# A four-layer image network on one core: layer 1 in pieces of 32 rows instead of 16, layer 0 in row pairs

## The chip, the cores and the metric

The kernel runs on one core of a Trainium2 chip. TensorE is PE here, VectorE is DVE, ScalarE is ACT, GpSimd is POOL; SyncE (SP) issues every transfer. PEld is PE's loading of weights. The metric is the device time of one execution in microseconds (us).

## The reference, cut to what matters

The input `x` has 8 images of 32 channels and 256 x 256 pixels, fp32. Four layers follow each other, and each has the form "x + layer(normalised x)", with a mean and a variance that the kernel gathers per channel or channel group over a whole image. So a layer of an image can't begin before the layer ahead of it has finished that image.

- Layer 0: a 1 x 1 convolution to `feat`, an average of `feat` over 5 x 5 regions, and a depthwise 5 x 5 convolution of `feat` with that average as its filter, zeros beyond the border. The kernel folds both convolutions into one 5 x 5 convolution of 32 x 32 channels, whose 25 taps differ by image.
- Layer 1, by far the largest: the input is normalised and rounded to whole numbers from -127 to 127 (`q`), and the output is a sum of absolute differences:

```
out[n, f, i, j] = -sum over c, kh, kw of | patch[n, c, i + kh, j + kw] - w[f, c, kh, kw] |     (3 x 3, 32 -> 32)
```

- Layer 2: a 3 x 3 convolution, 32 to 32 channels, with bias.
- Layer 3: four blocks of "FastKAN" (layernorm, 8 Gaussian bases per value, a matrix, plus SiLU times a matrix) on windows and on grids of pixels.

## The kernel before

**Layout.** An image's 256 rows are cut into 4 bands (`q` as an index, `NQ`) of 64 rows; a tile has 128 partitions, 32 channels of each band. A chunk `k` is 8 rows of each band; 8 chunks make an image.

**A planner writes the order.** The code does not issue instructions as it goes. Each step is a task with an engine, an estimated duration, the buffers that it reads and writes, and a rank; `Plan.run` plays all tasks and fixes the order on PE, DVE, ACT and SP before anything is issued. Each engine then works through its own list in that order. Layers of neighbouring images overlap: while layer 1 works on image b, layer 0 of image b + 1 and layers 2 and 3 of image b - 1 run beside it. `TURN`, `L0A`, `L0B`, `L3A`, `L3B` are the ranks, as fractions of an image.

**Layer 1** (`stage1`, `Pass`, `Parts`). Because |a - w| = 2 max(a - w, 0) - a + w, the sum splits into three. The large part is max(q - w, 0), one instruction per output channel and tap over all input channels: `Parts.distance`, on DVE at line 1133 (subtract, max) or, as a filler in ACT's gaps, at line 1135, where one ACT instruction makes half the rows. It writes a bf16 tile of kind `dv`, of which there are `NDV` = 3. PE then sums over the channels with a 128 x 32 selection matrix (`gather`, line 1155): eight matmuls of 512 columns, four side by side in the array. The second part is the box sum of q itself, the same for all outputs (also line 1155, source `qh`), nine gathers. The third is a constant, `wsum`.

A pass is one quarter of the rows of each band (`h`, `NH` = 4, `RH` = 16 rows) and one quarter of the outputs (`g`, `NG` = 4, `OG` = 8 outputs): 72 distances and 9 box-sum gathers into the accumulator `psA` (2 banks), to which PE adds the layer's own input with two fp32 identity matmuls (`residual`, line 1144). ACT evicts `psA` to `xr` (line 1202) and sums it; a second ACT instruction squares it (line 673) after a one-column shift on DVE (line 666). There is one `psA`, so the next pass's first gather waits for that eviction. There are 16 passes an image. `qh`, the rows of q with one more on each side, has two buffers of 18 rows, used in turn and loaded by SP (line 1174). `xr` is loaded (line 1193) and stored (line 1215) in four transfers of 128 KB.

**Layer 0** (`stage0`). For the first image alone a chunk is convolved with 32 x 32 tiles. For the others `one_block` loads one band's chunk four times (line 954), shifted by a row, a column and both, so that K = 128 holds 2 x 2 taps: nine taps (line 967) of four 128 x 32 fp32 matmuls into `psC`, one bank. DVE first clears the margins of the tile (lines 941 and 942). ACT evicts (line 989). There are 32 blocks an image, tiles of kind `x0`, 3 slots; if these are taken and enough of the shared `arena` is free, a block takes its tile there.

**Layers 2 and 3** use `psB` (4 banks) and groups of 16 matmuls of 32 x 32 tiles (`mm16`, line 631; layer 2 at line 1287; the scales of layer 3 at line 1426; variances at line 1394 with 128 x 32). Bases are made by ACT at lines 1530 and 1545 or by DVE at line 1535; they lie in `bas`, `arena` or, once layer 1 is over, `dv`. Where it serves, DVE does an eviction at line 1382.

Of the kernel before, what the change touches and what calls it, by code (L numbers as in the profile page):

```python
# [24 lines left out]
R = 8  # L25
# [23 lines left out]
KCOL = 7  # L49


C32, MG, MS, IDENT, MV, W0, CQ, RL, ONES, PAT = range(10)
NMAT = 10


EYE, CEN32, CEN16 = range(3)
VAR = 3
# [6 lines left out]
NSEL = 9 + W0T  # L64


BASE = 16 * (W + 2) // 2
XP = W + 4
XW = 12 * XP
NX = 3  # L70
NBAS, NSI = 2, 3
TURN = (0.05, 0, 0.12, 0.2, 0.071, 0.232, 0.274, 0.235, 0.5, 0.311, 0.737, 0.685, 0.891, 0.2)


def room():
    n = 13 * F + 3 * BASE - NBAS * BASE - NSI * F - NX * XW
    fixed = [("bas", NBAS * BASE, BASE), ("si", NSI * F, F), ("rs", F // 2, F // 4), ("xr", 3 * F // 4, 3 * F // 4)]
    return fixed + [("x0", NX * XW, XW), ("sb", n, 0)]

URGENT = 2  # L80
IDLE = 8.0
NDV = 3
SPARE = 512
WIDE_SPARE = 9216
BASE_SPARE = 0
HOLD = 1
L0A, L0B = -0.0321, 0.4065
L3A, L3B = 0.0072, 0.7303
# [6 lines left out]
NH = 4  # L95
RH = HB // NH
NG = 4
OG = C // NG
NJ = 4
NI = 2  # L100
# [19 lines left out]
class Plan:  # L120
# [57 lines left out]
    def fits(self, need, spare):  # L178
# [3 lines left out]
        for b in need:  # L182
            if b.kind in ("dv", "bas") and b.spill:
                b.kind = "dv" if self.places["dv"] else "bas"
# [208 lines left out]
class Pass:  # L393


    def __init__(self, plan, b, h, g, opened, parts):
        self.b, self.h, self.g, self.opened, self.parts = b, h, g, opened, parts
        self.terms = [(o, t) for t in range(9) for o in range(OG)]
        self.queue, self.rest = [], None
        self.sums = list(range(9))  # L400
        self.left = 9 + OG * 9
        self.ps = Buf("psA")
        self.ps.first, self.ps.left = self, 1
        self.added = self.done = False
        plan.passes.append(self)

    def piece(self, plan, e):

        if self.rest is None:
            d = Buf("dv")  # L410
            d.spill = self.b == 0
            if not plan.fits([d], 0):
                return None
            (o, t), lo = self.terms.pop(0), 0
            d.left = 3
        else:
            (o, t, d, lo), self.rest = self.rest, None
        hi = RH if e == "DVE" or lo else RH // 2
        if hi < RH:
            self.rest = o, t, d, hi  # L420
        elif not lo:
            d.left = 2

        def ended(_):
            d.made = getattr(d, "made", 0) + hi - lo
            if d.made == RH:
                self.queue.append((o, t, d))

        us = (0.13 + 1.075 * (hi - lo) / RH) if e == "DVE" else 0.12 + 3.575 * (hi - lo) / RH
        return plan.filler(e, us, lambda: self.parts.distance(self, e, d, o, t, lo, hi), [d], [d], ended)  # L430

    def on_pe(self, plan, urgent):
# [4 lines left out]
        late = (9 - len(self.sums)) * 9 < 9 * 9 - self.left or not (self.terms or self.rest or self.queue)  # L437
        if self.sums and len(self.queue) < URGENT and (late or not (urgent or self.queue)):
            t, us, bufs, n = self.sums.pop(0), 0.46, [], 1
            fn = lambda: self.parts.gather(self, None, None, t)  # L440
        elif self.queue and (len(self.queue) >= URGENT or not urgent):
            o, t, d = self.queue.pop(0)
            us, bufs, n = 0.46, [d], 1
            fn = lambda: self.parts.gather(self, d, o, t)
        elif not self.added and self.residual.over and (self.left < 20 or not urgent):
            us, bufs, n = 1.75, [], 0
# [18 lines left out]
def kernel(  # L465
# [26 lines left out]
    nc.sync.dma_start(tl[:, :W0T], sel[:, OG + 1 :])  # L492
# [31 lines left out]
    sel_b = const.tile([P, OG + 1, C], BF16, name="sel_b")  # L524
# [4 lines left out]
    with tc.tile_pool(name="prepp", bufs=2, space=PSUM) as ps:  # L529
# [7 lines left out]
        sel_f = prep((OG + 1) * C).rearrange("p (o c) -> p o c", c=C)  # L537
        nc.sync.dma_start(sel_f, sel[:, : OG + 1])
        nc.vector.tensor_copy(sel_b, sel_f)
        wi = prep(C * 9)  # L540
# [28 lines left out]
        nc.vector.memset(one_k, QSCALE)  # L569
        for g in range(NG):  # L570
            spread = prep(P)
            by_place = spread.rearrange("p (j o q) -> p o j q", j=NJ, o=OG)
            for i in range(NJ * NQ):
                nc.vector.tensor_copy(by_place[:, :, i // NQ, i % NQ], wo[:, g * OG : (g + 1) * OG])
# [7 lines left out]
    qh = [const.tile([P, RH + 2, W + 2], BF16, name=f"qh{i}") for i in range(2)]  # L582
    for i in range(2):
        nc.gpsimd.memset(qh[i][:, :, 0:1], 0.0)
        nc.gpsimd.memset(qh[i][:, :, W + 1 : W + 2], 0.0)
# [4 lines left out]
    tiny = const.tile([P, 350], F32, name="tiny")  # L590
    img = [
        {
            "x1": scratch.tile([NH, NJ, C, NQ, NI, 512], F32, name=f"x1_{b}"),
            "x2": scratch.tile([NH, NJ, C, NQ, NI, 512], F32, name=f"x2_{b}"),
# [42 lines left out]
    class Norm:  # L637


        def __init__(self, b, which, n, rank, last=None):  # L640
            at = 0 if which < 2 else 1 + b % 2
            t = tiny[:, at * 110 : at * 110 + 110]
            self.n, self.rank, self.last = n, rank, last
            self.mv = t[:, 68 : 68 + 2 * n].rearrange("p (n s) -> p n s", s=2)
            self.g = t[:, 76 : 76 + 2 * n].rearrange("p (n s) -> p n s", s=2)
            self.d = t[:, 84 : 84 + 2 * n].rearrange("p (n s) -> p n s", s=2)
            self.v = t[:, 92 : 92 + n]
            self.t = t[:, 96 : 96 + n]
            at = 330 + 2 * (5 * (b % 2) + which)
            self.m = tiny[:, at : at + 2]  # L650
            self.y = t[:, 104 : 104 + n]
# [4 lines left out]
            self.nsums = 2 * NH * n if n == 1 else NH * n  # L656
# [23 lines left out]
        def finish(self):  # L680
            n, average, last = self.n, MV if self.n > 1 else MG, self.last
# [3 lines left out]
            def first():  # L685
                mean, d, q = self.mv[:, :, 0], self.v, self.t
                for of, a, k in ((d, self.sums, self.nsums), (q, self.squares, 2 * NH * n if n == 1 else NH * n)):
# [8 lines left out]
            pv = lambda: psC[:, 0 : 2 * n].rearrange("p (n s) -> p n s", s=2)  # L696
# [17 lines left out]
            def third():  # L714
# [11 lines left out]
                if last is None:  # L726
                    nc.vector.tensor_copy(self.m, self.g[:, 0, :])

            plan.add("DVE", 2.8, third, r=[p], w=[small] + ([self.done] if last is None else []), rank=self.rank)
            if last is not None:  # L730

                p = Buf("psC")

                plan.add(
                    "PE", 0.6, lambda: nc.tensor.matmul(pv(), mat(last), self.g, start=True, stop=True),
                    r=[small], w=[p], rank=self.rank,
                )

                def fifth():
                    if n == 1:  # L740
                        nc.vector.tensor_copy(self.m, pv()[:, 0, :])
                        return
                    nc.vector.tensor_scalar(self.m, pv()[:, 0, :], col(GSEL), None, ALU.mult)
                    for i in range(1, n):
                        nc.vector.scalar_tensor_tensor(
# [1098 lines left out]
```

## Time and profile before

| | us |
|---|---|
| three runs, lowest, median, highest | 15038.8, 15039.77, 15045.56 |
| the profiled execution | 15035.73 |
| its span, first to last instruction | 15034.0 |
| DVE busy | 13135.5 |
| PE busy | 12664.4 |
| ACT busy | 11831.0 |
| HBM read and written, in MB | 1424.32 and 771.75 |

The page gives busy times of each engine over the span and the costliest groups of instructions: line, engine, operation, output and inputs, partitions x elements, count, then busy time in us and the mean of one in ns, then the engine's idle time ahead of them and what ended it. A view of waits lists who waited for whom, with total, number and longest. The windows view lists the stretch, its length, and busy time (and instructions) of PE, PEld, DVE, ACT and POOL, then the granted TensorE clock, the DMA share and GB/s. The timeline merges neighbouring instructions of a kind: start, duration, what, count, and in brackets the idle time before. A duration includes an end in which the next instruction may already have started, so a pace is read from start to start.

### The profile page before, as it was taken

The numbers are of one execution on the slowest core, as the hardware profiler recorded it, in microseconds if no ns is written. First come the engines' busy times: TensorE is split into PE (matmuls) and PEld (weight loads), VectorE is DVE, ScalarE is ACT, GpSimd is POOL, SyncE is SP. The second block draws the span as 40 slices with busy tenths as digits, with TensorE's granted clock in tenths as the row PEclk, the third lists the DMA queues.
The fourth block names the chain that finished last, engine by engine and source line by source line (L and its number), as shares of the span: only waits on it lengthen the run. The fifth ranks groups of instructions, "written<-read, shape, count | busy, mean of one in ns | idle before, by whom it ended". The sixth has DMA issues, their size and how long they took to land. (4 is left out here: it accounts for less than half of the span.)

```text
span 15034.0 us, 506670 instructions
## 1 busy us (share of the span) xinstructions
PE 12664.4 (84%) x231764; PEld 4345.4 (29%) x231764; DVE 13135.5 (87%) x12530; ACT 11831.0 (79%) x7586; POOL 32.3 (0%) x25
## 2 busy tenths in 40 slices
PE   6898978889878899889998899978998887866566
PEld 4333322223222232222332223322232222222122
DVE  1899899998999999999899998899989999975676
ACT  1899678896788868888688877888778888876567
POOL 0000000000000000000000000000000000000000
PEclk8999989999999999999999999989999999987677
DMA  4655566665766566765767658775677655455565
GB/s 120 120 131 119 132 158 152 144 147 136 175 157 148 139 144 156 175 157 142 172 161 181 158 123 182 178 172 132 149 170 181 145 127 122 125 143 132 144 149 134
DMA packets 2583263, 2229.00 MB, mean 148 GB/s; under 512 B 1436416, under 2 KB 2292992, under 8 KB 2506368
## 3 DMA queue, kind: packets, MB, share of 16 engines
q1 hardware_dynamic: 2581120, 2196.57, 61.8%
q8 instruction: 1815, 29.74, 0.9%
q14 instruction: 328, 2.69, 0.1%
HBM read 1424.32 MB, written 771.75 MB: 146 GB/s over the span
## 5 line engine op out<-in xcount | busy, mean ns | idle before, releaser
L1133 DVE TENSOR_SCALAR dv<-qh,w1q 128x4128 bf16<-128x4128 bf16 (+1 forms) x8897 | 10649.3, 1262 | 718.5 <-PE psA L1155 697.1
L1155 PE MATMUL psA<-dv,sel_b 128*32 128x512 bf16 x71304 | 5339.1, 393 | 1090.3 <-DVE dv L1133 858.5
L1155 PEld LDWEIGHTS <-sel_b 128*32 128x32 bf16 x82944 | 2128.1, 96 | 6106.5 <-issue 5138.8
L1530 ACT ACTIVATE bas<-arena,kb 128x2048 f32<-128x2048 f32 x1016 | 2009.2, 1996 | 449.9 <-PE psB L631 242.3
L967 PE MATMUL psC<-x,w 128*32 128x512 f32 x15768 | 1985.1, 596 | 21.1 <-ACT x L989 8.6
L1545 ACT ACTIVATE bas<-bas 128x2048 f32<-128x2048 f32 x1016 | 1926.9, 1899 | 0.4
L631 PE MATMUL psB<-bas,tl 32*32 32x512 f32 x35584 | 1424.9, 646 | 290.0 <-ACT bas L1545 99.5
L1135 ACT ACTIVATE dv<-qh,w1n 128x2064 bf16<-128x2064 bf16 x481 | 947.6, 2007 | 570.0 <-PE psA L1155 541.6
L1530 ACT ACTIVATE arena<-arena,kb 128x2048 f32<-128x2048 f32 x697 | 1388.5, 1993 | 4.9 <-DVE arena L1434 2.4
L1545 ACT ACTIVATE arena<-arena 128x2048 f32<-128x2048 f32 x697 | 1317.1, 1900 | 0.0
L631 PE MATMUL psB<-arena,tl 32*32 32x512 f32 x30240 | 1160.3, 609 | 104.3 <-ACT si L1618 49.5
L1434 DVE TENSOR_TENSOR arena<-psB,arena 128x2048 f32<-128x2048 f32 x280 | 639.7, 2284 | 149.9 <-PE psB L1426 147.6
L1618 ACT ACTIVATE si<-psB,cols_sb 128x2048 f32<-128x2048 f32 x189 | 371.4, 1965 | 501.3 <-PE psB L631 447.2
L1155 PE MATMUL psA<-qh,sel_b 128*32 128x512 bf16 x9216 | 677.7, 386 | 100.6 <-DMA qh<-q 84.4
L967 PEld LDWEIGHTS psC<-x,w 128*32 128x32 f32 x15768 | 501.6, 110 | 700.5 <-issue 401.7
L631 PEld LDWEIGHTS psB<-bas,tl 32*32 32x32 f32 x35584 | 360.9, 107 | 960.3 <-issue 425.1
L1377 ACT ACTIVATE arena<-psB 128x2048 f32<-128x2048 f32 x216 | 405.0, 1875 | 293.1 <-PE psB L631 292.9
L631 PE MATMUL psB<-si,tl 32*32 32x512 f32 x13984 | 608.7, 629 | 26.9 <-issue 7.0
L1287 PE MATMUL psB<-x,tl 32*32 32x510 f32 (+1 forms) x15360 | 584.9, 608 | 36.6 <-issue 36.5
L1385 ACT ACTIVATE arena<-arena 128x2048 f32<-128x2048 f32 x273 | 522.5, 1914 | 11.6 <-PE psV L1394 2.3
L1426 PE MATMUL psB<-rs,tl 32*32 32x512 f32 x8960 | 348.7, 641 | 145.2 <-DVE arena L1434 66.5
L631 PEld LDWEIGHTS psB<-arena,tl 32*32 32x32 f32 x30240 | 291.2, 103 | 549.5 <-issue 290.5
(211 smaller groups left out, 8697.1 us busy)
## 6 DMA issues: line engine op xcount, KB each, us to landing
x<-in_x_dram SPq DMA_DIRECT2D x850, 384.0 KB
arena<-y SPq DMA_DIRECT2D x128, 1024.0 KB
si<-sy SPq DMA_DIRECT2D x500, 256.0 KB
x<-x SPq DMA_DIRECT2D x492, 256.0 KB
x<-x SPq DMA_DIRECT2D x120, 1024.0 KB
arena<-x SPq DMA_DIRECT2D x68, 1024.0 KB
xr<-x SPq DMA_DIRECT2D x512, 128.0 KB
x<-xr SPq DMA_DIRECT2D x512, 128.0 KB
```

The lines of the kernel that those rows point to most:

```text
L631: nc.tensor.matmul(view(o[j * C : (j + 1) * C, i - first, :]), w_, src(rows, i, j), start=start, stop=stop)
L967: nc.tensor.matmul(psC[j * C : (j + 1) * C, :], w4[:, t, :], d[:, 2 * j + y : 2 * j + y + 2, z : z + W], start=t == 0, stop=False,)
L1133: nc.vector.tensor_scalar(dst, src, w1q[:, at : at + 1], 0.0, ALU.subtract, ALU.max)
L1135: nc.scalar.activation(dst, src, AF.Relu, bias=w1n[:, at : at + 1])
L1155: nc.tensor.matmul(psA[j * C : (j + 1) * C, i, :], sel_b[:, n, :], src[:, at : at + 2, t % 3 : t % 3 + W], **flags,)
L1287: nc.tensor.matmul(o[:, lo - 2 * j : hi - 2 * j, c0:c1], (wc if t == 4 else tl[:, W2T + t, :])[rows], d[rows, lo + dy + 1 : hi + dy + 1, c ...
L1377: lambda ps=ps, at=at: nc.scalar.activation(sb(c)[:, at], ps().rearrange("p s f -> p (s f)"), func, bias=shift),
L1385: square = plan.add("ACT", 1.82, lambda: nc.scalar.activation(sb(sq), sb(c), AF.Square), r=[c], w=[sq], rank=rk)
L1434: lambda ps=ps, at=at: nc.vector.tensor_tensor(sb(c)[:, at], ps().rearrange("p s f -> p (s f)"), sb(c)[:, at], ALU.mult),
L1530: lambda: nc.scalar.activation(sb(bas), sb(rb), AF.Square, bias=kb[:, n, k : k + 1]),
L1545: lambda: nc.scalar.activation(sb(bas), sb(bas), AF.Exp, scale=-1.0, bias=0.0 if sq.eng == "ACT" else kbsq[:, n, k : k + 1]),
L1618: nc.scalar.activation(sb(o), psB.rearrange("p s f -> p (s f)"), AF.Identity, bias=obias)
```

## The change

- Layer 1's piece is 32 rows (`NH` = 2, `RH` = 32) and two outputs (`NG` = 16, `OG` = 2): a distance is 8256 elements per partition, a gather 16 matmuls into one bank of `psA`, a pass 18 distances; there are 32 passes an image. `dv` has two tiles of 32 rows.
- q of a half image lies in one buffer of 34 rows, loaded in two parts. The last pass of a half image makes its distances rows 0 to 15 first, then 16 to 31; the first part of the load is released when the first are made, the second when all are. The first pass of the next half makes rows 0 to 13 first, then 14 to 31.
- The nine box sums are made once for each half image, into `psC`, and put away as two bf16 halves (`ss`, by ACT and by DVE). Each pass adds them with two bf16 identity matmuls beside the fp32 one for its input.
- Layer 0's block is one half of a chunk, two bands in two row groups of 64: each band's rows are loaded twice, shifted by one row, so K = 64 holds two rows of taps, and 15 taps of eight matmuls fill two banks of `psC`. The columns at the border are left out of the matmul instead of cleared in the tile; only blocks at the image's upper and lower border are still cleared.
- Outputs of layer 0 are kept in another channel order, so that a pass's two outputs lie where one transfer fetches or stores them; the sums of the norm are averaged and picked accordingly.
- `x0` has 2 slots, `bas` 1, `xr` 3 (of half the size); ranks and planner constants are set anew; ACT's piece as a filler stays 16 rows (`RA`), after `IDLE` = 16 us instead of 8.

```diff
-NX = 3
-NBAS, NSI = 2, 3
+NX = 2
+NBAS, NSI = 1, 3
-URGENT = 2
-IDLE = 8.0
-NDV = 3
+URGENT = 1
+IDLE = 16.0
+NDV = 2
+RA = 16
-NH = 4
+NH = 2
 RH = HB // NH
-NG = 4
+CUT = RH // 2
+NG = 16
 OG = C // NG
-NI = 2
+NI = 4
...
 def piece(self, plan, e):
-        hi = RH if e == "DVE" or lo else RH // 2
+        hi = z if e == "DVE" or lo > a else min(a + RA, z)
...
+            load = self.then[part]
+            if load is not None and not self.open[part]:
+                load.wait -= 1
...
 def one_block
-                for s in range(4):
-                    lo, hi = max(r0 - 2 + s // 2, 0), min(r0 + 10 + s // 2, H)
-                    nc.sync.dma_start(
-                        grid(slice(s * C, (s + 1) * C))[:, at : at + hi - lo, 2 - s % 2 : 2 - s % 2 + W], x[b, :, lo:hi, :]
-                    )
+                for n in range(4):
+                    i, s = divmod(n, 2)
+                    r0 = first(i) - 2 + s
+                    lo, hi = max(r0, 0), min(r0 + 12, H)
+                    rows = slice(n * C, (n + 1) * C)
+                    nc.sync.dma_start(
+                        sb(xt)[rows, (lo - r0) * W : (hi - r0) * W], x[b, :, lo:hi, :].rearrange("c r w -> c (r w)")
+                    )
...
+            if first(0) == 0 or first(1) + R == H:
+                plan.add("DVE", 0.6, clear, w=[xt], rank=rk - 0.03 * span, after=after)
...
                 for j in range(NJ):
-                    nc.tensor.matmul(
-                        psC[j * C : (j + 1) * C, :], w4[:, t, :], d[:, 2 * j + y : 2 * j + y + 2, z : z + W],
-                    )
+                    for i in range(2):
+                        rows = slice(i * 2 * C, (i + 1) * 2 * C)
+                        nc.tensor.matmul(
+                            o[:, :, c0:c1], w4[rows, t, :], grid(rows)[:, 2 * j + y : 2 * j + y + 2, c0 + dx : c1 + dx],
+                        )
...
 class Parts
-            src, dst = qh[ps.h % 2][:, t // 3 + lo : t // 3 + hi, :], place(d)[:, lo:hi, :]
+            src, dst = qh[:, t // 3 + lo : t // 3 + hi, :], place(d)[:, lo:hi, :]
...
         def residual(self, ps):
-            for i in range(NI):
-                nc.tensor.matmul(psA[:, i, :], mat(IDENT), sb(ps.xr)[:, i * 512 : (i + 1) * 512], **flags)
+            nc.tensor.matmul(psA, mat(IDENT), sb(ps.xr)[:, 0:FS], start=start, stop=False)
+            for i in range(2):
+                nc.tensor.matmul(psA, eye_b, halves(ps.ss, i), start=False, stop=stop and i == 1)
...
+        def total(self, h, t):
+            src = qh[:, t // 3 : t // 3 + RH, t % 3 : t % 3 + W]
+            for n, (j, w, v) in enumerate(by_unit(OG * NI, src)):
+                i = n // NJ
+                nc.tensor.matmul(psC[j * C : (j + 1) * C, 0], sel_b[:, w, :], v, ...)
...
 def stage1
+            for t in range(9):
+                plan.add("PE", 0.88, lambda h=h, t=t: Parts().total(h, t), r=qh_buf, w=[p], rank=b - SUMS)
+            plan.add("ACT", 0.57, lambda s=s: nc.scalar.activation(halves(s, 0), psC[:, 0], AF.Copy), r=[p], w=[s], ...)
+            low = plan.add("DVE", 0.7, lambda s=s: nc.vector.tensor_tensor(halves(s, 1), psC[:, 0], halves(s, 0), ALU.subtract), ...)
...
+                if g == 0 and (b or h):
+                    ps = Pass(plan, b, h, g, [loads[:1], loads[1:]], [0, CUT - 2, RH], Parts())
+                elif ends:
+                    ps = Pass(plan, b, h, g, [loads, loads], [0, CUT, RH], Parts())
+                else:
+                    ps = Pass(plan, b, h, g, [loads], [0, RH], Parts())
```

## The prediction

> **What bounds the kernel now.** I read the page first, then the busy time of each engine by stretches, the groups with shapes kept apart, the waits of DVE, and the timeline of a steady place.
>
> ```profile
> PE 12664.4 (84%) x231764; PEld 4345.4 (29%) x231764; DVE 13135.5 (87%) x12530; ACT 11831.0 (79%) x7586; POOL 32.3 (0%) x25
> ```
>
> No engine is full over the span, but the span has three parts: a start without layer 1 (0 to 425), eight images of layer 1 (425 to 13292), a tail with the last image's layers 2 and 3. In the middle:
>
> ```profile
> 2256.00:13160.00 10904.00, 9600.33 (x177656) 3119.22 (x177656) 10119.05 (x9356) 8937.41 (x5733) 24.71 (x13) 0.97 0.65 153
> 13292.00:15034.00 1742.00, 1084.76 (x21360) 394.28 (x21356) 1089.97 (x606) 1163.42 (x699) 0.00 (x0) 0.75 0.58 144
> ```
>
> After the stretch come PE, PEld, DVE, ACT. In the middle DVE is at 93%, PE at 88%, ACT at 82%; in the tail none is over 67%, so the tail is a chain of latencies. What DVE does in the middle, and on what it waits:
>
> ```profile
> L1133 DVE TENSOR_SCALAR dv<-qh,w1q 128x4128 bf16<-128x4128 bf16 x8448 | 10364.0, 1289 | 716.4 <-PE psA L1155 695.0 <-DMA qh<-q 6.6 <-issue 2.3
> L1133 DVE TENSOR_SCALAR dv<-qh,w1q 128x2064 bf16<-128x2064 bf16 x449 | 336.1, 750 | 2.1 <-PE psA L1155 2.1
> DVE dv L1133 <- PE psA L1155: 697.1, 681, 19.1
> DVE x L941 <- PE psC L967: 61.1, 5, 25.6
> ```
>
> So layer 1's distances on DVE set the end, and their only large wait is for a buffer that PE has not yet gathered. The timeline gives the true pace of both:
>
> ```profile
> 5999.07 12.13 DVE L1133 TENSOR_SCALAR dv<-qh,w1q 128x4128 bf16<-128x4128 bf16 x10
> ...
> 6012.15 19.36 DVE L1133 TENSOR_SCALAR dv<-qh,w1q 128x4128 bf16<-128x4128 bf16 x16 [0.95 <-PE psA L1155]
> ...
> 6027.96 0.62 PE L1155 MATMUL psA<-dv,sel_b 128*32 128x512 bf16 x8 [0.59 <-DVE dv L1133]
> 6028.51 1.14 PE L631 MATMUL psB<-arena,tl 32*32 32x512 f32 x32
> 6029.58 0.62 PE L1155 MATMUL psA<-dv,sel_b 128*32 128x512 bf16 x8
> ...
> 6033.61 0.61 PE L1155 MATMUL psA<-dv,sel_b 128*32 128x512 bf16 x8
> 6034.04 1.03 PE L967 MATMUL psC<-x,w 128*32 128x512 f32 x8
> 6034.90 0.61 PE L1155 MATMUL psA<-dv,sel_b 128*32 128x512 bf16 x8
> ```
>
> One distance: (19.36 - 12.13) / 6 = 1.205 us. A gather of 8 matmuls takes 0.43 us until the next may start (6033.61 to 6034.04), a layer 0 tap 0.86 (6034.04 to 6034.90). Together 1.29: where PE has one tap per gather it is slower than DVE.
>
> **DVE: the larger pieces.** Between 2064 and 4128 elements the duration grows by 1289 - 750 = 539 ns, so 4128 elements stream for 1.078 us and 1.205 - 1.078 = 0.127 us is paid per instruction. A piece of 32 rows (8256 elements, no row of it here) is 2.156 + 0.127 = 2.283 us by this line against 2.41 for two pieces; the bounds are nothing saved, and 0.211 (what the durations, not the pace, extrapolate to at no elements). I take the pace. There are 8 x 2 x 16 x 18 = 4608 such pieces. ACT made the equal of 333 of the 9216 small ones (666 halves), so DVE keeps about 4441: 4441 x 0.127 = -564. At 15 changes of half image the last pass and the first one after it are cut in two, 18 more instructions each: 15 x 36 x 0.127 = +69. Net **-495**.
>
> **DVE: layer 0's clears** go but for two an image: 224 x (0.078 + 0.088) = -37. They stand in DVE's queue and wait there for a buffer that PE's taps must free (the L941 line, and 7.2 us for blocks in the arena): -68. **-105.** New on DVE: 12 more one-column shifts an image at 0.16 (L722's 159 ns) and 16 subtractions of 512 columns at about 0.7 (L1382 takes 1.22 for 1024): **+26**. DVE in all **-574**.
>
> **PE** is not the bound, so its terms count through DVE's waits. Box sums: 9216 matmuls become 2304, 6912 / 8 x 0.43 = -372; this work now stands just behind each pass change, where PE is behind. Residual: the fp32 identity matmuls stay 256; 512 bf16 ones come, half of 0.43 each, +110, and 128 more visits at 0.33 (below), +42. Layer 0: 2016 taps at 0.86 = 1734 become 15 x 16 x 7 = 1680, since a tap now does two blocks. No row shows a tile of 64 x 32. The nearest are the 128 x 32 tap beside a gather (0.86) and the 32 x 32 group: 0.55 + 1.07 from gather to gather (6027.96 to 6029.58), which is 0.33 more than 0.43 + 0.86. So a tap costs 0.86 to 1.19, the whole 1445 to 1999; I take 1.07 without a change before each: 1798, +64. PE in all -156 (-509 to +45): no relief to count on, no harm.
>
> The Trainium skill (TensorEngine Tiling, Key Properties) says that changing the tiling mode, not just the tile, drains the TensorE, which speaks against a third tile shape among the gathers; the row of 0.33 us agrees with it, and at 0.33 for each of 1680 taps it would make of the layer 1999 us instead of 1445.
>
> **ACT.** The pass's eviction and square come 256 times over 512 columns instead of 128 times over 1024: 256 x (0.676 + 0.192 + 0.71 + 0.19) - 128 x (1.104 + 0.194 + 1.141 + 0.190) = +116 (the 0.71 between 1.141 and 2.000 by the same line). Layer 0 evicts 112 x 1.30 instead of 224 x 0.87: -49. Sums +11. +78 on an engine at 82%; other ACT work hides it in part: between 0 and 78, I take **+39**.
>
> **The waits.** DVE starts a piece when a buffer is free. With three buffers of 16 rows, small piece 2m needs the gather of 2m - 3; with two of 32 rows, large piece m needs that of m - 2, whose second half is the same 2m - 3. So half of the checks vanish, and the others see a gather that ends 0.43 later. Bounds: 697 / 2 = -349, and 681 x 0.43 = +293. I take **0**, since DVE asks faster of a PE with unchanged work. Pass changes double to 256. From the last piece to the first gather behind it the path was 0.43 + eviction 1.30 + 0.43 against three pieces (3.6 us); now 0.86 + 0.87 + 0.86 against two (4.57): more room for ACT's current instruction each time. PE itself waits 107.4 us for these evictions; bounds 0 and +107, I take **+50**.
>
> **One buffer for q.** While its first half is reloaded, DVE works 18 x 1.205 = 21.7 us on the second; while the second is reloaded, 18 x (0.127 + 14/16 x 1.078) = 19.3 us on the first 14 rows. Each part is about 1.1 MB; 1 MB takes 5.6 to 10.3 us in the chain's DMA pieces, plus SP's queue. That hides it. But the sums then need both parts, psC (which layer 0 holds for a block) and 9 turns of PE before the first pass may end: 0 to 10 us at 15 changes, I take 3: **+45**. Queued behind q's load on SP are all later transfers, as before.
>
> The Trainium skill (Trainium Kernel Development and Optimization, Best Practices) asks for double buffers to overlap DMA with compute; that rule is against the single q. By it 2 x 15 loads of up to 10 us would stand open, +300; the trace shows 6.6 us of DVE waiting for q with two buffers and cannot show one.
>
> **Off the path.** Layer 0's second loads halve (896 of 384 KB to 448), the pass's transfers go from 4 of 128 KB to one of 256, layer 2's from 12 per chunk to 3: about 1500 fewer issues on SP, none of which DVE waits for now. x0 falls from 3 slots to 2, so a block's load is no longer ahead of the block before; layer 0 has a whole image of 1650 us for some 240 taps, so 0. The tail loses one of about eleven base buffers and gets another order of ranks: -50 to +50 (3% of 1742), 0.
>
> **Sum.** -574 + 39 + 0 + 50 + 45 = -440. From the profiled span 15034: 14594. That execution took 15035.73, the median of the three is 4 above it: **14600**.
>
> **Rivals.**
> *PE's lateness decides (slower).* From a finished piece to a buffer's need, PE may be late by two small pieces less a gather, 2.41 - 0.43 = 1.98 us; now by one large piece less its gather, 2.283 - 0.86 = 1.42. Every wait of today grows by 0.56 (681 x 0.56 = 381), taps at 1.19 add 265 of PE work, gates +107: about +700 on DVE's waits, 15034 - 574 + 700 + 84 = 15244, call it 15240. For it: the 88% of PE, and waits of 5 to 19 us where PE stands in order behind ACT. Against it: the halved checks and the sums gone. It decides once DVE's waits for PE pass some 1190 us.
> *The waits fall with the pieces.* They halve, and pass changes cost nothing: 15034 - 574 - 349 + 84 = 14195, call it 14200. For it: box sums now stand among the late gathers.
> *The long instruction saves nothing.* If 8256 elements take 2.41, -564 is gone and the 69 stays: about 15160. Two sizes on one line speak against it.
> *ACT binds.* RA = 16 makes ACT's own pieces twice as long and +116 is dense; the gain is eaten to within 30 us of 15040.
>
> **How the numbers follow.** Forecast 0.52 (its own range 14400 to 14850), waits halved 0.20, PE late 0.20, no saving 0.04, ACT 0.04. Faster 0.72, slower 0.24; same 0.04, where "same" is within 0.2%, about 30 us, what a measurement of this kernel can tell. The range 14250 to 15150 leaves out about a tenth on each side: the lower part of the second case, the upper half of the third.
>
> **What would show it.** Right: a 128x8256 group of some 4400 on DVE at a pace near 2.28 us, DVE's waits for PE between 400 and 1000 us, no DVE wait for q over 50, the last distance near 12850 us and a tail near 1740. Wrong: waits for PE over 1190; taps spaced over 1.2 us; DVE waits for q's loads, or a first pass of a half image longer than its fellows; a tail over 1800; images of layer 1 at 1650 us or more.

## The result and the profile after

Twenty executions of each kernel: before 15046.77 us (15031.92 to 15068.18), after 15086.63 (15061.86 to 15103.31). The ratio of the means is 1.0022, 95% interval 1.0015 to 1.0029: slower by 0.22% (0.26% by the medians), where 14600 was forecast. The profiled execution after has a span of 15085.5, 51.5 more than before.

The page's busy times, the windows of the middle and of the tail (columns as explained above), and the groups of distances with shapes apart:

```profile
PE 12714.9 (84%) x236108; PEld 4221.4 (28%) x236108; DVE 12629.1 (84%) x8049; ACT 11599.1 (77%) x7506; POOL 16.9 (0%) x23
```

```profile
2256.00:13160.00 10904.00, 9576.27 (x177844) 3041.51 (x177833) 9540.32 (x5812) 8788.93 (x5884) 13.55 (x13) 0.95 0.57 141
13383.00:15085.00 1702.00, 1070.70 (x21006) 385.16 (x21002) 1046.59 (x584) 1164.77 (x701) 0.00 (x0) 0.75 0.57 143
```

```profile
L1169 DVE TENSOR_SCALAR dv<-qh,w1q 128x8256 bf16<-128x8256 bf16 x3771 | 8670.7, 2364 | 264.6 <-PE psA L1187 251.6 <-DMA qh<-q 5.0 <-issue 1.3
L1169 DVE TENSOR_SCALAR dv<-qh,w1q 128x4128 bf16<-128x4128 bf16 x611 | 772.4, 1293 | 163.1 <-PE psA L1187 162.3
```

DVE has 506 us less to do, and in the middle it fell from 93% to 87%, while PE stayed at 88% and ACT fell from 82% to 81%. The engine that was called the bound was relieved, and the end did not move. DVE's waits say where the room went:

```profile
DVE dv L1169 <- PE psA L1187: 593.9, 732, 9.5
DVE x L1140 <- ACT x L1134: 389.7, 17, 49.4
...
DVE dv L1169 <- DMA qh<-q: 63.3, 5, 28.6
```

The first wait was expected, and is 103 us smaller than before. The second is new in size; before, the same two lines waited 16 us:

```profile
DVE x L1109 <- ACT x L1103: 16.3, 5, 7.0
```

L1134 and L1140 (L1103 and L1109 before) make q for the next image out of layer 0's output. DVE stands there because layer 0 of the next image is not done. The windows of one image and of the change that follows it:

```profile
6425.00:7980.00 1555.00, 1435.36 (x26985) 457.25 (x26986) 1458.34 (x852) 1245.08 (x847) 2.56 (x2) 0.98 0.57 142
7980.00:8324.00 344.00, 215.13 (x3846) 63.03 (x3846) 54.17 (x109) 308.15 (x184) 0.00 (x0) 0.72 0.69 165
```

Within the image DVE is busy for 1458 of 1555 us, as full as ever, and PE for 1435. In the 344 us behind it, it works 54, while ACT works 308. DVE's timeline shows the last distances, the wait for q, and the first distances of the next image:

```profile
7978.00 2.50 DVE L1169 TENSOR_SCALAR dv<-qh,w1q 128x4128 bf16<-128x4128 bf16 x2 [0.76 <-PE psA L1187]
7994.43 0.48 DVE L981 MEMSET x<- 32x512 f32 x1 [13.94 <-DMA x<-x]
...
8123.09 1.23 DVE L1140 TENSOR_SCALAR x<-x 128x2048 bf16<-128x2048 f32 x1 [38.25 <-ACT x L1134]
...
8288.69 1.23 DVE L1140 TENSOR_SCALAR x<-x 128x2048 bf16<-128x2048 f32 x1 [39.66 <-ACT x L1134]
...
8323.94 2.23 DVE L1169 TENSOR_SCALAR dv<-qh,w1q 128x3612 bf16<-128x3612 bf16 x2 [5.77 <-DMA qh<-q]
```

And ACT's, with the last eviction of layer 0 (L1021) and the first q (L1134) among layer 3's squares (L1588) and exponentials (L1603):

```profile
8071.88 3.69 ACT L1603 ACTIVATE arena<-arena 128x2048 f32<-128x2048 f32 x2
8075.48 1.09 ACT L1021 ACTIVATE x<-psC,cc 128x1024 f32<-128x1024 f32 x1
...
8119.10 1.97 ACT L1676 ACTIVATE si<-psB,cols_sb 128x2048 f32<-128x2048 f32 x1 [4.15 <-PE psB L664]
8120.97 2.08 ACT L1134 ACTIVATE x<-x,cc 128x2048 f32<-128x2048 f32 x1
```

From the trace I added up, image by image, the time from the first distance of layer 1 to the last, and the time from there to the next image's first (images divided where the last eviction of each starts):

| | eight images, us | seven changes, us | last distance ends | from there to the end |
|---|---|---|---|---|
| before | 12864 | 2 | 13291 | 1743 |
| after | 12171 | 780 | 13380 | 1705 |

Four changes, from the fourth image on, make up 772 of the 780 us: 108, 343, 138 and 183. Before, there is not one stretch of over 40 us without a distance.

The same traces read from the other end: when layer 1's last eviction of an image started, and when the first store of layer 3's output of that image was issued.

| image | 1 | 2 | 3 | 4 | 5 | 6 | 7 | 8 |
|---|---|---|---|---|---|---|---|---|
| before: last eviction | 1671 | 3321 | 4969 | 6648 | 8308 | 10057 | 11742 | 13292 |
| first store | 2318 | 4115 | 5856 | 7600 | 9354 | 11118 | 12781 | 14174 |
| behind by | 647 | 794 | 887 | 952 | 1046 | 1061 | 1039 | 882 |
| after: last eviction | 1635 | 3187 | 4780 | 6320 | 7984 | 9970 | 11703 | 13383 |
| first store | 2269 | 4103 | 5866 | 7605 | 9351 | 11149 | 12843 | 14227 |
| behind by | 634 | 916 | 1086 | 1285 | 1367 | 1179 | 1140 | 844 |

The stores come at much the same times in both kernels, 1744 us from image to image before and 1762 after (first to seventh). Layers 0, 2 and 3, which run beside layer 1, did not get faster; I call them **the chain**. Why it is 18 us an image slower after was not found. Already before, it falls back behind layer 1 (whose images end 1679 us apart) from 647 to 1061 us. After, layer 1 runs away from it faster, to 1285 us at the fourth image; there layer 0, a part of the chain, is late too, and layer 1 must wait for it. Each image of the chain is seven steps of some 190 us from one output unit of layer 3 to the next (of eight; second to seventh image, 190.0 before and 189.9 after), and a **handover** of some 385 us from the last unit to the next image's first (522 before and 494 after between the first two images). The 190 us are no fixed length: in the eighth image, beside which no layer 0 or 1 runs and for which more buffers are free, a unit takes 122 us in both kernels.

### The profile page after: what moved, and what is told of

It is laid out like the page before. It is cut to its first block, busy times and chain, and to the rows that moved or that the text cites. A ratio compares the mean times of both kernels' runs of the same rounds, so it can differ in the third digit from the quotient of the medians.

```text
span 15085.5 us, 504492 instructions
## 1 busy us (share of the span) xinstructions
PE 12714.9 (84%) x236108; PEld 4221.4 (28%) x236108; DVE 12629.1 (84%) x8049; ACT 11599.1 (77%) x7506; POOL 16.9 (0%) x23
## 5 line engine op out<-in xcount | busy, mean ns | idle before, releaser
L1169 DVE TENSOR_SCALAR dv<-qh,w1q 128x8256 bf16<-128x8256 bf16 (+3 forms) x4907 | 10092.4, 2115 | 669.9 <-PE psA L1187 593.9
L1588 ACT ACTIVATE arena<-arena,kb 128x2048 f32<-128x2048 f32 x1202 | 2388.9, 1990 | 42.1 <-PE psB L664 40.5
L1603 ACT ACTIVATE arena<-arena 128x2048 f32<-128x2048 f32 x1202 | 2260.4, 1897 | 0.2
L664 PE MATMUL psB<-arena,tl 32*32 32x512 f32 x49280 | 1962.7, 630 | 284.6 <-ACT arena L1603 140.8
L995 PE MATMUL psC<-x,w 64*32 64x510 f32 (+2 forms) x21360 | 1387.7, 598 | 13.4 <-issue 9.1
L1588 ACT ACTIVATE bas<-arena,kb 128x2048 f32<-128x2048 f32 x488 | 974.7, 1997 | 331.9 <-PE psB L664 191.1
L664 PE MATMUL psB<-bas,tl 32*32 32x512 f32 x17696 | 739.8, 658 | 249.9 <-ACT bas L1603 115.9
L1603 ACT ACTIVATE bas<-bas 128x2048 f32<-128x2048 f32 x488 | 926.0, 1898 | 0.6
L1171 ACT ACTIVATE dv<-qh,w1n 128x4128 bf16<-128x4128 bf16 x137 | 507.2, 3722 | 338.9 <-PE psA L1187 328.7
L1443 ACT ACTIVATE arena<-arena 128x2048 f32<-128x2048 f32 x275 | 525.9, 1912 | 11.7 <-DVE arena L1440 3.7
L1345 PE MATMUL psB<-x,tl 32*32 32x510 f32 (+2 forms) x13056 | 507.5, 613 | 22.8 <-issue 22.7
```

What stands on the lines that cost most here:

```text
L664: nc.tensor.matmul(view(o[j * C : (j + 1) * C, i - first, :]), w_, src(rows, i, j), start=start, stop=stop)
L995: nc.tensor.matmul(o[:, :, c0:c1], w4[rows, t, :], grid(rows)[:, 2 * j + y : 2 * j + y + 2, c0 + dx : c1 + dx], start=t == K + mid, stop=F ...
L1169: nc.vector.tensor_scalar(dst, src, w1q[:, at : at + 1], 0.0, ALU.subtract, ALU.max)
L1171: nc.scalar.activation(dst, src, AF.Relu, bias=w1n[:, at : at + 1])
L1345: nc.tensor.matmul(o[:, lo - 2 * j : hi - 2 * j, c0:c1], (wc if t == 4 else tl[:, W2T + t, :])[rows], d[rows, lo + dy + 1 : hi + dy + 1, c ...
L1443: square = plan.add("ACT", 1.82, lambda: nc.scalar.activation(sb(sq), sb(c), AF.Square), r=[c], w=[sq], rank=rk)
```

## The experiments

Theory: the chain sets the pace, before as after, and layer 1 can only be as early as the chain lets it. Rivals: the two slots of `x0` hold up layer 0 alone; the new layer 1 saves nothing; one engine is full.

**Layer 3 left out** of both kernels: layer 2 stores the output, and ACT makes no filler pieces.

```diff
-IDLE = 16.0        # before: 8.0
+IDLE = 1e9
-    nc.sync.dma_start(im["x3"][k], sb(xo, F))
+    by_block(lambda p, q: nc.sync.dma_start(out[b]...[k, q], sb(xo, F)[p]))
-    ends = stage3(b - 1, norm3, x3buf, b + L3A, L3B)
```

> The kernel after, with layer 3 left out (layer 2's result is stored as the output) and ACT making no distances from image 1 on. Chain theory (the layers beside layer 1, with layer 3's 200 us a unit on ACT, have become the bound, and layer 1 only waits for its next q): without layer 3 the kernel is bound by layer 1 on DVE and ends near 11700, at least 400 below the same cut of the kernel before. Slot theory (layer 0 is late because its tiles have two slots): layer 0's lateness stays, with image changes that still stand open by 100 to 400 us. DVE theory (layer 1 in larger pieces is in itself no faster): within 150 us of the same cut of before.

> The kernel before with the same cut: layer 3 left out, no distances on ACT from image 1 on. Chain theory: near 12250, 400 to 700 above the cut kernel after, since here layer 1 alone is the bound in both. DVE theory: within 150 us of the cut kernel after.

After 11938.69, before 12251.55: 313 us less. Changes of image: 16 us in all after, 11 before. The windows over the same steady 3000 us and DVE's largest wait over the whole run, first of after, then of before:

```profile
8000.00:11000.00 3000.00, 2031.84 (x25036) 762.34 (x25035) 2846.68 (x1528) 216.59 (x356) 5.20 (x4) 0.86 0.12 29
```

```profile
DVE dv L1169 <- PE psA L1187: 456.6, 532, 4.9
```

```profile
8000.00:11000.00 3000.00, 2091.84 (x26540) 701.32 (x26540) 2937.92 (x2545) 187.63 (x214) 178.81 (x4) 0.85 0.13 29
```

```profile
DVE dv L1133 <- PE psA L1155: 254.7, 269, 6.5
```

Where nothing of layer 3 runs, DVE is full (98%) before, and the new layer 1 is faster. So the gain exists, and the gaps belong to layer 3's presence. It is smaller than the 400 that was expected; DVE, with two large buffers, waits 202 us more for PE (95% busy).

**Layer 1 fed with the image before**: q and its input are those of an image earlier, so it never waits for the next image's layer 0.

```diff
-    def stage1(b, x1buf, qbuf):
-        im = img[b]
+    def stage1(b, a, x1buf, qbuf):
+        im = {**img[a], "x2": img[b]["x2"]}
...
-            norm2, x2buf = stage1(b, *x1q)
+            norm2, x2buf = stage1(b, *given)
+            given = (b, *x1q)
```

> The kernel after, in which layer 1 of each image from 1 on takes q and its input from the image before, so that layer 0 of an image has a whole image more of time; all work is still done. Slot theory: the 900 us at image changes fall to some 350 and the time falls by 500 to 650, to about 14500. Chain theory: the image changes close too, but layer 3's chain ends when it did, and the time stays within 200 of 15080; DVE's freed time shows up as a longer stretch behind layer 1.

15173.63, ratio to before 1.0078 (1.0049 to 1.0108). The changes shrink to 21 us in all, the last distance ends at 13028, 352 us earlier, and the end comes 87 us later: 

```profile
13030.00:15170.00 2140.00, 1314.62 (x26154) 466.85 (x26146) 1313.77 (x702) 1479.75 (x881) 0.00 (x0) 0.74 0.58 144
```

The tail takes 2147 us for 1705. What layer 1 no longer waits for, the chain takes at the end. DVE's wait for q was therefore a symptom: taking it away moves the same lateness. Part of it shows up inside layer 1 too, where DVE now waits for the box sums of a half image (89 us in the kernel after):

```profile
DVE ss L1241 <- ACT ss L1237: 216.0, 9, 69.3
```

**One tap of nine left out of layer 1 in the kernel before.** By the trace that takes 1122 us of DVE's busy time and, since the tap's gathers go too, 456 us of PE's.

```diff
-        self.terms = [(o, t) for t in range(9) for o in range(OG)]
+        self.terms = [(o, t) for t in range(8) for o in range(OG)]
```

> The kernel before, with 8 of layer 1's 9 taps: one ninth of DVE's distances, some 1220 us of DVE work, is left out. DVE theory (the prediction's own bound): the time falls by 1000 or more. Chain theory: the kernel before was already nearly balanced, so it falls by less than 500, and image changes open in it as in the kernel after.

14757.54, ratio 0.9802 (0.9774 to 0.983): 302 us less than the kernel before beside it (15059.13), for 1122 of relief. Now the kernel before shows the same picture, four changes of some 240 us each and 

```profile
DVE dv L1133 <- PE psA L1155: 721.2, 651, 18.3
DVE x L1109 <- ACT x L1103: 370.4, 26, 24.6
```

with 1732 us from image to image in the chain (before 1744). The first store comes 174 us earlier (2144 for 2318), so more than half of the gain is made in the first image, before there is a chain to wait for. So in the kernel before the chain was already the slower stream; DVE's 93% belonged to a neighbour that ran only a little faster.

**What is the chain's pace made of?** Two of eight exponentials left out (after, and before), and the matmuls of two bases left out (after):

```diff
                 square(k)
-                exp(k - 1)
-            exp(GRID - 1)
+                if k < 7:
+                    exp(k - 1)
```

```diff
-            for k in range(GRID):
+            for k in range(6):
                 main(k)
```

> The kernel after, with two of the eight exponentials of each layer 3 block left out (the last two bases stay squares): 2 x 4 x 64 x 1.9 = 973 us less on ACT, nothing else changed. If ACT's capacity sets layer 3's pace of about 200 us a unit: a unit falls by 15, and the time by 400 to 700. If layer 3's pace is set by the order of its steps through the one psB, or by PE: less than 200.

> The kernel after, with PE's matmuls of two of the eight bases of each layer 3 block left out: 2 x 4 x 64 x 1.07 = 548 us less on PE, all of ACT's work still done. If PE or the time that psB is held sets the pace: 300 to 500 less. If ACT's capacity does: within 150 of 15090.

> The kernel before with the same cut as the ACT one (two of eight exponentials left out, 973 us of ACT). If the chain beside layer 1 already set the time before the change, it falls here too, but by less than in the kernel after (layer 1 at some 1650 us an image is next): 150 to 350. If DVE's layer 1 set it: only what the tail gives, some 60 to 120.

14979.74, ratio 0.9957 (0.9938 to 0.9977): 107 us less than after, for 867 us of ACT's busy time. 14884.08, ratio 0.9895 (0.9866 to 0.9924): 202 less for 506 of PE's. The kernel before without the exponentials: 15020.76, ratio 0.9984 (0.9973 to 0.9995), 31 less for 675 of ACT's. A unit went from 190 us to 186, 185.5 and (before) 182. Neither engine's work alone is the pace. The last run misses both of its expectations: if the chain alone had held the kernel before, more should have come off. In its trace layer 1 ends 72 us later (13363) and the tail is 102 us shorter (1641): the two streams of the kernel before lay close together, and each holds the end when the other is relieved.

**Layer 0 as before (K = 128) with the new layer 1.**

> Layer 1 as after, layer 0 as before: four loads per block, K = 128, nine taps, margins cleared by DVE, one bank of psC, 32 blocks an image; x0 stays at 2 slots (of 3120 words, 96 words fewer for the arena). Chain theory: row pairs made the work beside layer 1 lighter on SP, ACT and DVE, so without them layer 0 is later still and the time rises by 200 to 600 over 15090, in the image changes. If 64-row tiles among the gathers are what costs (the drain): it falls by 100 to 300.

15585.64, ratio 1.0361 (1.0331 to 1.0392): 499 us slower than after, with 1393 us of changes, the chain at 1834 per image, and PE busy 12775.3 us, 60 more than after. So the row pairs are no harm; without them the new layer 1 would have cost 3.6%. This layer 0 has twice the blocks in the same two slots; whether the slots or the blocks' work are at fault was not taken apart. The row pairs with the old layer 1 were not tried: their accumulators would take nine banks, and both kernels use eight.

**psB held longer.** No work changes; a block of layer 3 takes the accumulator one basis earlier.

```diff
-HOLD = 2           # before: 1
+HOLD = 1           # before: 0
```

> One constant of the kernel after: a block of layer 3 may take the four-bank accumulator psB as soon as its second basis is made (HOLD = 1, as in the kernel before), not its third (HOLD = 2). No work changes; psB is only held about one basis, some 3.7 us (one square and one exponential), longer per block of some 29.4 us. Theory 'the chain of layers 0, 2 and 3 beside layer 1 goes by psB': about 200 blocks lie beside layer 1, so up to +740 us, and at least +250 with what the rest of the schedule makes up, with the stretch from one unit of layer 3 to the next at 210 to 225 us in place of 200. Rival 'the chain goes by ScalarE's or TensorE's capacity': within 60 us of the kernel after, units at 200 us. Rival 'the chain goes by the order alone, each block by its own latency': the blocks start a basis earlier, so the same or up to 150 us less.

> The same step the other way in the kernel before, whose constant is 1: HOLD = 0, psB is taken once the first basis is made. Theory 'psB': +250 to +700 us against the kernel before, units longer by 10 to 25 us. Rival 'capacity': within 60 us. Rival 'order alone': the same or up to 150 less. If this kernel slows and the kernel after with HOLD = 1 doesn't, or the other way round, psB isn't what the two have in common.

After: 15363.8, ratio 1.0209 (1.0192 to 1.0226). Before: 15227.48, 1.0117 (1.01 to 1.0134). By the trace, psB was held per block 30.9 us for 29.4, and 31.5 for 30.2 (first matmul into it to the end of the instruction that reads it): some 1.5 and 1.3, not 3.7. Times some 200 blocks beside layer 1 that is 300 and 260, for 277 and 174 measured. The size fits; the place doesn't. Units stayed at 190 and 192 us, and handovers grew (after: 456 and 526 us at the fourth and fifth, for 386 and 406), with one change of image of 956 us. The two new orders after, further down, hold psB just as long (30.4 and 30.8 us a block, the second with this very `HOLD = 1`) and are 200 us and more faster than the kernel after. So the cost may be that of these two orders alone; that holding psB longer costs in itself, or that psB sets a unit's length, is not shown.

**Layer 0 with 8 of its 15 taps.**

```diff
-            for t in [K + mid] + [t for t in range(3 * K) if t != K + mid]:
+            for t in [K + mid] + [t for t in range(3 * K) if t != K + mid][:7]:
```

> The kernel after with 8 of the 15 matmul taps of layer 0 (left out: the other 7, so its sums are not the reference's). That takes some 800 us from TensorE, 11200 of 24000 matmuls at about 70 ns of busy time each. Theory 'the chain of layers 0, 2 and 3 is one sequence that ends late at each image, and layer 0 is only a part of it beside the other two': -150 to -250 us against the kernel after, with the changes of image 4 to 8 (now 167 to 431 us) shorter but not gone, and the time from one image's first output to the next near 1715. Rival 'the two slots of x0 hold layer 0, and layer 0 alone is late': layer 0 is done in half the time, the changes close to 70 us, and the time falls by 500 us or more. Rival 'TensorE's capacity': -500 or more too, but with shorter units of layer 3 (under 190 us).

14882.14, ratio 0.9887 (0.987 to 0.9903): 204 us less than after, with 661 of PE's busy time gone. The changes closed altogether (21 us), as the rival of the slots expected and the theory did not, and layer 1's last distance came at 12812, 568 earlier. But the end came only 204 earlier, and the tail took 2068 us: the chain again (1742 us an image, where the theory had 1715), and the 500 or more of both rivals, the slots and TensorE's capacity, did not come.

**Six of eight bases** of every block, squares, exponentials and matmuls; and **four of nine taps of layer 2**, whose chunks hold psB in the handover.

```diff
-            bases.extend(Buf("bas", F) for _ in range(GRID))
+            bases.extend(Buf("bas", F) for _ in range(6))
...
-            for k in range(GRID):
+            for k in range(6):
                 main(k)
```

```diff
-            taps = [4, 0, 1, 2, 3, 5, 6, 7, 8]
+            taps = [4, 0, 1, 2]
```

> The kernel after with six of the eight bases of each block of layer 3 (left out: squares, exponentials and matmuls of the last two). Taken one by one, the exponentials gave -107 us and the matmuls -202, with units of 186 and 185.5 us for 190. Theory 'ScalarE, TensorE and psB's hold limit a unit together, each close behind the other': taking all three gives clearly more than the sum of -309: -450 to -700, units of 160 to 172 us, and the changes of image 4 to 8 close (under 100 us without a distance in all, for 772). Rival 'the order or the handover between images sets the pace, and a unit's work counts by the piece': -250 to -350, units over 180 us.

> The kernel after with four of the nine taps of layer 2 (left out: five taps, 320 groups of 1.07 us, -342 us of TensorE), whose chunks hold psB some 20 us each in the stretch between the last unit of one image and the first of the next (some 385 us). Theory 'that stretch is a sequence through psB, on the path': the 43 us per image come off it: handovers near 345, -200 to -320 us. Rival 'the stretch waits on something else (norms, loads, the next image's layer 0), and layer 2 is hidden in it': within 80 us of the kernel after.

Six bases: 14623.43, ratio 0.9717 (0.9701 to 0.9734), 463 less than after. That is more than the two parts, 309, but ACT lost 1647 us here, the squares among it, which neither part left out, and PE 540; so it does not show that the engines stand close behind one another. A unit is still 178 us where 160 to 172 were expected, and 443 us of changes remain. Light layer 2: 15016.03, ratio 0.9975 (0.9966 to 0.9985), 71 less, within the rival's bound: the handover is not a row of layer 2's chunks. What the handover is made of stays open.

**A new order for the same work.** The ranks and the planner's constants are set anew, and VectorE, where it has nothing of its own, takes a square or an eviction meant for ACT; once more for the kernel after, and with the same means for the kernel before. The first of the three, in excerpt:

```diff
+                    if best is None and e == "DVE":
+                        for t in ready[e]:
+                            ...
+                            if t.eng != e and not (t.gate and not t.gate(self)) and self.fits(t.need, t.spare):
+                                best = t
...
-IDLE = 16.0
+IDLE = 24.0
-L0A, L0B = -0.0128, 0.4602
-L3A, L3B = 0.0588, 0.669
+L0A, L0B = 0.0294, 0.0088
+L3A, L3B = -0.4684, 0.6553
...
-            norm3, x3buf = stage2(b - 1, *later, b + 0.0, 0.1, [])
+            norm3, x3buf = stage2(b - 1, *later, b + L2A, L2B, [])    # -0.0242, 0.1674
```

> The kernel after, same work, with another order: the ranks at which an image's stages are due are set anew (layer 0 due earlier in layer 1 of the image before, the 14 starting offsets, the idle threshold of ScalarE 24 for 16 us), and VectorE, where it has nothing of its own, takes a square or an eviction that was meant for ScalarE. Theory 'the gain in layer 1 is real and is lost to the chain beside it, whose late end makes VectorE wait at the change of image': an order in which layer 0 ends before the last distances closes the changes from 167-431 to some 70-150 us; since the chain's own pace stays, it gives 100 to 350 us: 14750 to 14990. Rival 'the chain's pace of 1745 us per image is fixed by its work, whatever the order': within 60 us of the kernel after, changes as long as they are, only in other places.

> The kernel before, same work, with the means of e12: constants of the order set anew (starting offsets, ranks of layers 0, 2 and 3, idle threshold 4 us, one base buffer and four staging buffers, the room kept free), and VectorE, where it has nothing of its own, takes a square or an eviction meant for ScalarE. Theory 'before, VectorE and the chain were both full, so no order can give much; the change made room on VectorE that only a new order can use': within 100 us of the kernel before, 14950 to 15100. Rival 'the gain of e12 is that of a better order, whatever the layer 1': -120 us or more, as e12 against the kernel after (-200), so 14850 to 14930.

> The kernel of e12 with other constants of the order (psB taken after two bases, the shared box sums and layer 2 due earlier and later by a tenth of an image, the filler on ScalarE in pieces of 8 rows, idle threshold 12 us). Theory 'the chain is the limit now, and what is left is how tightly its stages follow each other': another 20 to 100 us less than e12, 14780 to 14865, with the time from image to image at 1685 to 1705 us for e12's 1707. Rival 'psB taken a basis earlier costs as in e9': slower than e12, 14920 or more.

The two orders after: 14884.84, ratio 0.9887 (0.9873 to 0.9902), and 14842.26, ratio 0.9861 (0.9846 to 0.9876). The kernel before: 15039.74, ratio 0.9995 (0.9985 to 1.0005). The windows of the same middle as above, of the first order after and of the kernel before with its new order:

```profile
2256.00:13160.00 10904.00, 9631.63 (x181462) 3097.61 (x181458) 10246.80 (x6021) 8663.20 (x5822) 10.38 (x13) 0.97 0.57 143
```

```profile
2256.00:13160.00 10904.00, 9491.49 (x175096) 3088.33 (x175100) 10327.88 (x9337) 8927.83 (x5682) 29.66 (x13) 0.97 0.64 152
```

and the squares that DVE takes over in the first, with its wait for the next image's q:

```profile
L1608 DVE SCALAR_TENSOR_TENSOR arena<-arena,kb 128x2048 f32<-128x2048 f32 x268 | 622.0, 2347 | 52.8 <-PE psB L679 35.8 <-PE psV L1467 15.9
L1608 DVE SCALAR_TENSOR_TENSOR bas<-arena,kb 128x2048 f32<-128x2048 f32 x117 | 274.8, 2349 | 72.4 <-PE psB L679 70.8
```

```profile
DVE x L1155 <- ACT x L1149: 10.5, 4, 8.1
```

DVE makes 472 squares (with 87 into `dv`) for 310, is back at 94% in the middle, and its wait for q falls from 390 us to 11. The chain's period falls to 1707 us, its handovers to some 350. The second order gains 43 more, but in the tail (1560 us for 1648), not in the period (1705), where it was expected. The kernel before gains nothing by its new order (one was run), though DVE makes 485 squares for 327 there too. So the change is worth about 1.3%, by 14842.26 against 15039.74, but only with a new order. The ranks and the moved squares were not tried apart: that the gain is DVE's freed time, given to the chain, is how I read the traces, and is not shown.

## Why the prediction was wrong

The step that failed is the one on top, "layer 1's distances on DVE set the end", and with it "Off the path": "layer 0 has a whole image of 1650 us for some 240 taps, so 0". The 93% of DVE and its small waits were read as the bound. But the chain beside it was the slower of the two, 1744 us an image against 1679. Taking 1122 us from the bound of that reading gave 302 (the kernel before with eight taps). And layer 0 was not free: it is part of the chain, and layer 1 waited for it at four changes of image, 772 us in all. I looked for a chain of latencies only in the tail, where DVE has nothing to do. The first stores of layer 3 beside the ends of layer 1, image by image, would have shown in the trace of before that layer 1 was running away from what follows it.

The terms themselves, by their own steps:

- *The larger pieces.* The pace is right. DVE's timeline after:

```profile
5999.19 13.76 DVE L1169 TENSOR_SCALAR dv<-qh,w1q 128x8256 bf16<-128x8256 bf16 x6
...
6019.54 11.47 DVE L1169 TENSOR_SCALAR dv<-qh,w1q 128x8256 bf16<-128x8256 bf16 x5
```

  13.76 - 11.47 = 2.29 us, for 2.283. The page's 2364 ns less 2 x 1289 would have given 214 ns saved per pair by durations; the pace gives 0.12.
- *DVE in all*: -506, for -574. ACT made the equal of 260 pieces of 16 rows, for 333: some 73 x 1.2 = 88 us that DVE had to make itself.
- *ACT*: its busy time fell by 232, where +78 was summed. The sum took the fillers as given; ACT's distances went from 948 + 368 to 507 + 455 us.
- *PE*: +51, for -156. A layer 0 tap is some 0.86 us to the next tap (0.88 in the median of the whole trace), and each change to or from a gather adds 0.12 to 0.15:

```profile
6011.70 1.94 PE L995 MATMUL psC<-x,w 64*32 64x508 f32 x32
...
6013.57 1.06 PE L1187 MATMUL psA<-dv,sel_b 128*32 128x512 bf16 x16
...
6014.55 0.18 PEld L995 LDWEIGHTS psC<-x,w 64*32 64x32 f32 x16 [0.43 <-issue]
```

  Two taps take 6013.57 - 6011.70 = 1.87 = 1.72 + 0.15, a gather of 16 until the next tap 0.98 = 0.86 + 0.12. With 1226 visits of layer 0 in the trace, 1680 x 0.86 + 1226 x 0.27 = 1776, for the 1798 that I took. The rule of the Trainium skill (TensorEngine Tiling, Key Properties) that a change of mode drains agrees; it comes per visit, not per tap, so the 1999 that was worked out with it did not come true.
- *The waits*: 697 to 594, for 0 expected: fine in the whole kernel, where DVE no longer pushes. Without layer 3 they rose by 202, so the term was too kind to the two buffers.
- *One buffer for q*: 45 was taken, the sums included. DVE waits 63 us for the loads, 5 times, and 89 us for the box sums, where its own part of putting them away stands in its queue:

```profile
DVE ss L1241 <- ACT ss L1237: 89.2, 6, 36.9
```

  So the term was too small by 107 us, most of it the sums. Without layer 3 the same two waits are 5 and 11 us. The rule of double buffers of the Trainium skill (Trainium Kernel Development and Optimization, Best Practices) was worked out to 300 for the loads; the measurement decides for the smaller cost.
- *Sum.* Layer 1's images became 693 us shorter, from first distance to last, of which part is other DVE work that moved into the changes; -440 was forecast. Of the signals named, the pieces, the pace, the waits for PE, the images (1521 us) and the tail (1705) came out as "right". DVE's waits for q's loads, 63 us, lay over the 50 given. The last distance came at 13380, where 12850 was given, and the text had no line for a wait at the change of image.

The rivals named PE, the gates, the long instruction and ACT, all inside layer 1. None had another layer as the bound. The case "ACT binds", at 15040 and with 0.04, comes nearest in time, by luck: its reason was another. In the sum of the case "PE's lateness", 381, 265 and 107 are 753, not about 700; nothing hangs on it. The measurement does lie inside the range, 14250 to 15150, because PE's lateness had stretched it.

## What to carry to other kernels

Before an engine's busy share is read as the bound, take each stream of work that runs beside it and write down its period: here the first store of each image, 1744 us, against 1679 for the images of the stream that looked like the limit. A cut on the faster of two streams buys little (1122 us gave 302), and shows up as a wait at the place where they meet. Closing the wait itself (the old q) was no gain; a new order, which among other things moved squares to DVE, was.

## What the runs showed of the hardware

A change between the array's shapes costs little here: 0.27 us per round trip between 128 x 32 gathers and 64 x 32 taps, and consecutive taps of eight 64 x 32 matmuls follow each other in 0.88 us (median over the trace after), for 0.86 of the four 128 x 32 matmuls of a tap before. In the change of image where DVE worked 54 of 344 us, TensorE was granted 0.72 of its clock, for 0.98 in the image before (the windows above): it was also the less busy of the two stretches, 63% for 92%.
